# A graph attention block: tile 2 of the last head turned by DMA, one pool of banks, an x tile in another bank, and layer 2's own logits by way of VectorE

## The chip, the cores and the metric

The kernel runs on one core of a Trainium2 chip. The metric is device microseconds of one execution; of several executions the median is compared. A core has five engines with instruction streams of their own: TensorE (PE in the profile; its weight loads are shown apart as PEld), VectorE (DVE), ScalarE (ACT), GpSimd (POOL) and SyncE (SP), which here issues most of the DMA transfers. The engines wait for one another by semaphores. Matrix products land in PSUM banks, from which ScalarE or VectorE take them to SBUF.

## The reference

Two graph attention layers over 512 nodes with 768 features, a residual and a layer norm. Layer 1 has 8 heads of 768 features, layer 2 has one. All is fp32.

```python
def gat_layer(x, W, a_s, a_d, b, edge_index, concat):
    h = (x @ W).reshape(n, H, C)
    alpha_s = einsum('nhc,hc->nh', h, a_s)
    alpha_d = einsum('nhc,hc->nh', h, a_d)
    e = leaky_relu(alpha_s[src] + alpha_d[dst], 0.2)
    m = segment_max(e, dst);  e = exp(e - m[dst])
    alpha = e / (segment_sum(e, dst)[dst] + 1e-16)
    out = segment_sum(h[src] * alpha[:, :, None], dst)
    return out.reshape(n, H * C) + b
h = elu(gat_layer(x, W1, a_src1, a_dst1, b1, edges, True))
out = gat_layer(h, W2, a_src2, a_dst2, b2, edges, True)
x = layernorm(x + out)
```

## The kernel before

The edges are counted once, by products of one-hot tiles (L804, L789, L830), into a dense 512x512 table `cnt`, in which an entry is the number of edges between two nodes. After that each head is dense: the projection x @ W1 of the head, a 512x512 table of logits by four tiles of 128 destination rows, a softmax weighted by the table, the product of the softmax with the projected features, ELU, and the head's share of the projection of layer 2, which is summed over heads into `h2`.

The large products are done with fewer multiplications than the plain form. By halves there are seven steps P1 to P7 per product, by thirds fifteen, P0 to P14. Each step multiplies sums of blocks (made by VectorE, ScalarE or by accumulating DMAs) into a PSUM bank, and its `empty` then moves the bank to SBUF, by a ScalarE copy or by a VectorE addition. Halves of the projections are at L445 (helper `product`), thirds at L527, the attention products at L1099 and, for the first and the last head, in `near_first` (L1139), which takes destination nodes 0 to 255 ahead of the others: its first steps P1 and P2 need the softmax of tiles 0 and 1 alone, and the sums of `right_sums` (L1072 to L1075) need all four tiles. An fp32 matmul runs as two passes, so a matmul of the code shows as two weight loads and two matmuls.

Order. Each engine executes its instructions in the order in which the program issues them. The order is written out by hand: while the matmuls of step n are issued, the functions listed in `plan[n]` are issued to the other engines. The last head has a `plan` of its own (L1406 to L1411).

The softmax tiles lie with destinations on the partitions and must be transposed into `PT` for the product with the features. Two ways exist. `turn` (L1020, L1021): four TensorE transpositions into a `tr` bank and a ScalarE copy into `PT`; the tile has then been scaled by `scale` (L1301, ScalarE; the reciprocal comes from VectorE, L1011 and L1012). `turn_out` and `turn_in`: ScalarE scales the tile (L1028) and parts its 4-byte words into two halves of 16 bits (L1031), SP issues a transposing DMA (L1033), and when it has landed ScalarE joins the halves in `PT` (L1036). In the last head tiles 0 and 1 go by DMA and tiles 2 and 3 by TensorE.

PSUM. Banks come from pools and are taken in turn; a matmul that starts a new tile waits until the last reader of that bank's earlier tile is done. While the edges are counted there are a pool `mm0` of three banks and a pool `held` of two, used by P1 of the first projection and its overlays; afterwards these are closed and one pool `mm` of five opens. `tr` has two banks, `bc` has one, first used by the warming matmuls at the start (L292) and later for the broadcast rows of logits.

The start. `turn_x` (L327, L328) transposes blocks of x by TensorE into a bank of `mm0` and copies them to `xT` by ScalarE. Four of these calls stand behind position 3 of the first projection; the bank of the third is freed by VectorE's L672. VectorE's L425 to L428 then make sums of x blocks.

Layer 2's logits. A row of 512 logits per kind, source and destination, is accumulated by TensorE into the bank `rows` at four positions of 32 partitions (L1535), then copied by ScalarE into `row2` (128x512, L1564). `pick` does two things with it: L1570 spreads the source row over all partitions, and L1572 collects the destination logits into four columns, one per tile of 128 nodes, by four matmuls whose weights are 128x128 blocks of `row2` and whose moving operand is one column of `picks`. VectorE copies the four columns to `own2` (L1575), and ScalarE needs them for the first tile of logits (L723). The VectorE addition L570, behind L1575 in VectorE's order, empties the bank that P4 of layer 2's projection waits for. `fold` (L1530) is VectorE work between them. L1626 is the final product.

Of the kernel before, what the change touches and what calls it, by code (L numbers as in the profile page):

```python
# [39 lines left out]
def gat_pass(  # L40
# [42 lines left out]
    ohp = counting.enter_context(tc.tile_pool(name="onehot", bufs=1))  # L83
    tr = ctx.enter_context(tc.tile_pool(name="tr", bufs=2, space=bass.MemoryType.PSUM))
    bc = ctx.enter_context(tc.tile_pool(name="bc", bufs=1, space=bass.MemoryType.PSUM))
    mm = counting.enter_context(tc.tile_pool(name="mm0", bufs=3, space=bass.MemoryType.PSUM))
    held = counting.enter_context(tc.tile_pool(name="held", bufs=2, space=bass.MemoryType.PSUM))

    def row_bcast(ap_row):
        return bass.AP(tensor=ap_row.tensor, offset=ap_row.offset, ap=[[0, P], [1, D]])  # L90
# [215 lines left out]
    ones = const.tile([P, 1], F32, name="ones")  # L306
    nc.vector.memset(ones, 1.0)

    picks = const.tile([P, 2], F32, name="picks")
    for j in range(2):  # L310
        nc.vector.tensor_reduce(picks[:, j:j + 1], ident.rearrange("p (j k) -> p k j", k=32)[:, j, :], axis=AX.X,
                                op=ALU.add)
    far = const.tile([P, 1], F32, name="far")
    nc.vector.memset(far, -NO_EDGE)
    tiny = const.tile([P, 1], F32, name="tiny")
# [4 lines left out]
    xT = keep.tile([P, DC, N], F32, name="xT")  # L320


    def turn_x(t, r):

        ps = mm.tile([P, 512], F32, name="mm")
        for k in range(HK):
            nc.tensor.transpose(ps[:, k * P:(k + 1) * P], x_sb[:, t, (r * HK + k) * P:(r * HK + k + 1) * P], ident)  # L327
        nc.scalar.copy(xT[:, r * HK:(r + 1) * HK, t * P:(t + 1) * P],  # L328
                       ps[:, :HALF].rearrange("p (k n) -> p k n", n=P))
# [322 lines left out]
    def first_projection(h, XA, B_, between):  # L652


        HS[h] = hs = hpool.tile([P, NT, D], F32, name="hs")
        new_alpha(h)
        bank = {}

        def step(p, over, i, out, op):
            def multiply():  # L660
                if over is None:
                    bank[p, i] = (held if p == "P1" else mm).tile([P, 512], F32, name="held" if p == "P1" else "mm")
                else:
                    bank[p, i] = bank[over, i]
                product(bank[p, i], XA, B_, p, i, over is None)

            def empty():
                ps, o = bank[p, i][:, :HALF], out(i)
                if op is None:
                    nc.scalar.copy(o, ps)  # L670
                else:
                    nc.vector.tensor_tensor(o, o, ps, op=op)  # L672
            return multiply, empty, op is not None

        steps = [
            ("P1", None, lambda i: hs[:, i, L], None),
            ("P2", None, lambda i: hs[:, i, L], ALU.add),
            ("P5", None, lambda i: hs[:, 2 + i, R], None),
            ("P3", "P5", lambda i: hs[:, i, R], None),
            ("P6", "P1", lambda i: hs[:, i, R], ALU.subtract),  # L680
            ("P7", "P1", lambda i: hs[:, 2 + i, R], ALU.subtract),
            ("P4", "P1", lambda i: hs[:, 2 + i, L], None),
        ]

        def firsts():
            for k in range(HK):
                if k == HK - 1:
                    between()
                for i in range(2):
                    if k == 0:  # L690
                        bank["P1", i] = held.tile([P, 512], F32, name="held")
                    nc.tensor.matmul(bank["P1", i][:, :HALF], XA["P1"][:, k, i * P:(i + 1) * P], B_["P1"][:, k, :],
                                     start=k == 0, stop=k == HK - 1, skip_group_check=True)

        items = [step(p, over, i, out, op) for p, over, out, op in steps for i in range(2)]
        for i, multiply in enumerate((firsts, lambda: None)):
            items[i] = (multiply, *items[i][1:])
        return items
# [66 lines left out]
    if not general:  # L765
# [76 lines left out]
                    done.add(t)  # L842


        turns = {3: [(2, 0), (3, 0), (2, 1), (3, 1)]}
        sums = const.tile([P, 2 * NT + 2], F32, name="sums")
        wholes = len(items)

# [14 lines left out]
        for n, batch in enumerate(batches):  # L863
            fresh = sorted({c // quarter for c in batch} - made)
            made.update(fresh)
            if n == 0:
                waiting = [lambda k=k: destinations(k) for k in fresh]
            else:
                first = ahead_of.get(n, [])
                head = 1 if n == 1 else len(waiting)  # L870
                here = None
                if n + 1 == len(batches):
                    (k,), (before, *rest) = fresh, waiting
                    before()
# [12 lines left out]
            items_here = max(wants[n] - pos if n < len(wants) else 0, 1)  # L887
            share = len(ahead) // (items_here + 1) if n == 0 else -(-len(ahead) // items_here)
            for f in masks:
                f()  # L890
            waiting, masks = [], []
            for f in extra.pop(n, []):
                f()
            while n < len(wants) and pos < wants[n]:
                if pos == wholes:
                    pairs = projection(1, XA, B1)
                    items += [(m, e, False) for m, e in pairs[:4]]
                multiply, empty, on_vector = items[pos]
                multiply()
                if on_vector:  # L900
                    waiting.append(empty)
                else:
                    empty()
                pos += 1
                for t, r in turns.get(pos, []):
                    turn_x(t, r)
                if pos == 1:
                    nc.scalar.activation(nidx, low, AF.Copy, bias=0.5)
                part = 0 if n == 0 and pos == 2 else share
                for c in ahead[:part]:  # L910
                    one_hot(c, True)
                del ahead[:part]
            for c in ahead:
                one_hot(c, True)
            if n == 2:
                turn_b1()
            if n == 0:
                ((k,),) = [sorted({c // quarter for c in batches[1]} - made)]
                made.add(k)
                destinations(k)  # L920
                waiting.pop()()
            uncounted += batch
            if n + 1 == len(batches):
                for t in range(NT):
                    half(t, 0)()
            if n == 2 or n + 1 == len(batches):
                count(uncounted, n > 2)
                uncounted = []
# [57 lines left out]
    counting.close()  # L986


    mm = ctx.enter_context(tc.tile_pool(name="mm", bufs=5, space=bass.MemoryType.PSUM))
    late = ctx.enter_context(tc.tile_pool(name="late", bufs=1))  # L990
    h2 = late.tile([P, NT, D], F32, name="h2")
    pass_ = late.tile([P, 2, 2 * TH], F32, name="pass")
# [310 lines left out]
    for h in range(H - 1):  # L1303
# [75 lines left out]
        else:  # L1379
# [14 lines left out]
            def sum_up(*names):  # L1394
                return [gsums[p] for p in names]

            def at(f, *args):
                return [lambda: f(*args)]
# [8 lines left out]
            if last:  # L1407
                plan = {0: finish[:1], 1: finish[1:] + sum_up("P12") + at(score, 0), 2: sum_up("P9", "P7"), 3: sum_up("P1"),
                        4: sum_up("P6") + at(scored, 0) + at(score, 1), 5: sum_up("P14"), 6: sum_up("P10") + at(scored, 1) + at(score, 2),
                        7: at(out_by_dma, 0) + sum_up("P5"), 8: sum_up("P11") + at(scored, 2) + at(score, 3), 9: at(out_by_dma, 1),  # L1410
                        10: at(scored, 3), 11: at(scale, 2) + sum_up("P3"), 12: third_sum + at(turn_in, 0) + at(scale, 3), 13: at(turn_in, 1)}  # L1411
                AA, lsums = left_sums(H - 1, pass_.rearrange("p j n -> p (j n)"))
                plan[13] += lsums[:2]
                plan[14] = lsums[2:3]
# [8 lines left out]
                for f in attend:  # L1423
                    also(13, f)
            for n, (multiply, empty) in enumerate(pairs):
                if last and n > 12:
                    turn(q[n - 11], n - 11)
                multiply()
                for f in plan.get(n, []):
                    f()  # L1430
# [97 lines left out]
    def fold(parts):  # L1528
        for part, i, op in parts:
            nc.vector.tensor_tensor(part, part, u2[:, i, :], op=op)  # L1530
# [31 lines left out]
        add_rows(al2[:, :, t], ident, t, slice(t * P, (t + 1) * P), False, True)  # L1562
    row2 = work.tile([P, N], F32, name="nr")
    nc.scalar.copy(row2, rows[:, :N])  # L1564
    fold(parts[:2])
    own = tr.tile([P, 512], F32, name="tr")

    def pick():
        BC[H] = bc.tile([P, 512], F32, name="bc")
        nc.tensor.matmul(BC[H][:, :N], picks[:, 0:1].to_broadcast([P, P]), row2, start=True, stop=True)  # L1570
        for t in range(NT):
            nc.tensor.matmul(own[:, t:t + 1], row2[:, t * P:(t + 1) * P], picks[:, 1:2], start=True, stop=True)  # L1572

    pairs[7][0](pick)
    nc.vector.tensor_copy(own2, own[:, :NT])  # L1575
# [105 lines left out]
```

## Time and profile before

| | us |
|---|---|
| runs | 615.61, 614.91, 615.52 |
| median | 615.52 |
| profiled execution | 615.07 |
| its span | 613.0 |
| PE busy | 604.9 (99% of the span) |
| DVE busy | 525.3 (86%) |
| ACT busy | 335.4 (55%) |
| POOL busy | 145.5 (24%) |
| granted TensorE clock, mean | 0.998 |

The span runs from the first to the last instruction of the record; the profiled execution's own time is 2.07 us more. In the timeline a row has the start, the busy time, the engine, the line, the operation with output and inputs, how many instructions it groups, and in brackets how long the engine stood idle before it and which instruction of which engine ended that idle time.

### The profile page before, as it was taken

What the parts mean: (1) busy time and instruction counts of PE and PEld (TensorE: products, weight loads), DVE (VectorE), ACT (ScalarE), POOL (GpSimd) and SP (SyncE); (2) the same over time, 40 slices, a digit from 0 to 9 for tenths busy, and PEclk for the clock granted to TensorE, in tenths of its full rate; (3) what the DMA queues carried; (4) which work ended last, traced back from release to release, by engine and by line L of the source; (5) the groups of instructions that cost most, each with busy time, mean ns of one, the idle gap of its engine ahead of it and who ended that gap; (6) DMA issues with size and microseconds to landing.
All of it is one profiled execution on the core that took longest, in us unless ns stands there. A gap on an engine that the chain in (4) does not pass through costs nothing.

```text
span 613.0 us, 8592 instructions
## 1 busy us (share of the span) xinstructions
PE 604.9 (99%) x2772; PEld 481.9 (79%) x2772; DVE 525.3 (86%) x1149; ACT 335.4 (55%) x628; POOL 145.5 (24%) x182
## 2 busy tenths in 40 slices
PE   9999999999999999999999999999999999999995
PEld 5665775558888888888888888888888888885553
DVE  7999889887999879977898879977898878978785
ACT  5669776803675165823766164932757056753360
POOL 3310101032431332422431332412342303110000
PEclk9999999999999999999999999999999999999999
DMA  8992949699999998999899999999789994790032
GB/s 293 317 214 56 292 83 314 142 330 313 209 170 242 254 240 210 151 313 255 184 179 240 235 249 227 144 324 223 177 193 204 299 284 70 165 262 4 18 78 81
DMA packets 107292, 126.24 MB, mean 206 GB/s; under 512 B 41526, under 2 KB 87530, under 8 KB 106474
## 3 DMA queue, kind: packets, MB, share of 16 engines
q1 hardware_dynamic: 74813, 90.24, 48.5%
q0 software_dynamic: 32064, 35.00, 36.7%
q8 instruction: 24, 0.39, 0.3%
q10 hardware_dynamic: 365, 0.40, 0.2%
q14 instruction: 26, 0.21, 0.1%
HBM read 97.22 MB, written 2.90 MB: 163 GB/s over the span
## 4 chain that ended last, share of the span: by engine, by line
PE 97%; DVE 2%; ACT 1%; issue 0%; DVEq 0%
PE mm L527 47%; PE mm L445 19%; PE mm L1099 18%; PE mm L1139 6%; PE mm L1626 3%; PE held L445 2%; PE bc L292 1%; DVE os L804 0%; PE tr L830 0%; DVE odw L789 0%; PE tr L1535 0%; DVE here L784 0%; ACT hs L484 0%; PE tr L1020 0%; PE mm L327 0%
## 5 line engine op out<-in xcount | busy, mean ns | idle before, releaser
L533 ACT ACTIVATE hs<-mm 128x512 f32<-128x512 f32 x30 | 17.9, 596 | 83.7 <-PE mm L527 83.3
L1099 PE MATMUL mm<-PT,hs 128*128 128x256 f32 x216 | 52.5, 379 | 0.0
L736 ACT ACTIVATE q<-q,nmax 128x512 f32<-128x512 f32 x32 | 23.1, 721 | 49.0 <-DVE nmax L732 48.9
L540 DVE TENSOR_TENSOR hs<-hs,mm 128x512 f32<-128x512 f32 x45 | 30.9, 687 | 18.5 <-PE mm L527 18.1
L1099 PEld LDWEIGHTS mm<-PT,hs 128*128 128x128 f32 x216 | 41.0, 190 | 5.8
L538 POOL DMA_DIRECT2D h<-pass x22 | 26.7, 1307 | 75.9 <-ACT pass L537 75.0
L540 DVE TENSOR_TENSOR h<-h,mm 128x512 f32<-128x512 f32 x56 | 38.3, 684 | 5.8 <-PE mm L527 5.6
L1036 ACT COPY PT<-zr 128x1024 uint16<-128x1024 uint16 x34 | 39.4, 1158 | 4.8 <-DMA zr<-nr 3.2
L527 PE MATMUL mm<-w2r,xT 128*128 128x256 f32 x160 | 37.8, 379 | 0.0
L527 PE MATMUL mm<-w2r,gT 128*128 128x256 f32 x160 | 37.0, 379 | 0.0
L1099 PE MATMUL mm<-pS,gS 128*128 128x256 f32 x144 | 37.0, 379 | 0.0
L136 POOL DMA_DIRECT2D w1t<-in_L_gnn_W_dram x18 | 30.1, 1970 | 25.8 <-DVE pS L1072 25.8
L527 PE MATMUL mm<-w1t,hs 128*128 128x256 f32 x144 | 34.1, 380 | 0.0
L527 PE MATMUL mm<-w1r,hs 128*128 128x256 f32 x144 | 34.0, 379 | 0.0
L527 PE MATMUL mm<-w1r,gS 128*128 128x256 f32 x144 | 34.0, 379 | 0.0
L527 PEld LDWEIGHTS mm<-w2r,xT 128*128 128x128 f32 x160 | 30.4, 190 | 4.1
L527 PEld LDWEIGHTS mm<-w2r,gT 128*128 128x128 f32 x160 | 30.4, 190 | 4.1
L136 POOL DMA_DIRECT2D w1r<-in_L_gnn_W_dram x12 | 14.5, 1208 | 80.4 <-DMA w1r<-in_L_gnn_W_dram 45.7
L527 PEld LDWEIGHTS mm<-w1t,hs 128*128 128x128 f32 x144 | 27.3, 190 | 3.9 <-ACT absent L537 0.2
L1099 PEld LDWEIGHTS mm<-pS,gS 128*128 128x128 f32 x144 | 27.4, 190 | 3.7
L527 PEld LDWEIGHTS mm<-w1r,gS 128*128 128x128 f32 x144 | 27.3, 190 | 3.7
L527 PEld LDWEIGHTS mm<-w1r,hs 128*128 128x128 f32 x144 | 27.2, 190 | 3.8
(328 smaller groups left out, 1555.4 us busy)
## 6 DMA issues: line engine op xcount, KB each, us to landing
w2r<-in_L_gnn_W_dram SPq DMA_DIRECT2D x48, 384.0 KB
w1r<-in_L_gnn_W_dram SPq DMA_DIRECT2D x43, 384.0 KB
w1t<-in_L_gnn_W_dram SPq DMA_DIRECT2D x24, 256.0 KB
h<-pass POOLq DMA_DIRECT2D x22, 256.0 KB, 6.6
gT<-xd SPq DMA_DIRECT2D x5, 1024.0 KB
w1t<-in_L_gnn_W_dram POOLq DMA_DIRECT2D x18, 256.0 KB, 6.8
a_s<-in_L_gnn_a_src_dram SPq DMA_DIRECT2D x8, 384.0 KB
a_d<-in_L_gnn_a_dst_dram SPq DMA_DIRECT2D x8, 384.0 KB
```

Of the source, the lines that this page charges most:

```text
L136: nc.gpsimd.dma_start(o, i, accum_op=ALU.add)
L292: nc.tensor.matmul(idle[:, :cols], zeros[:, :P], zeros[:, :cols], start=True, stop=True)
L445: nc.tensor.matmul(ps[:, :HALF], A_[p][:, k, i * P:(i + 1) * P], B_[p][:, k, :], start=start and k == 0, stop=k == HK - 1, skip_group_chec ...
L527: nc.tensor.matmul(bank[chain][:, i * TH:(i + 1) * TH], A_[p][:, k, i * P:(i + 1) * P], B_[p][:, k, :], start=first and i == k == 0, stop= ...
L533: nc.scalar.activation(out(o), ps, AF.Copy, scale=sign)
L538: nc.gpsimd.dma_start(out(o), part, accum_op=ALU.add)
L540: nc.vector.tensor_tensor(out(o), out(o), ps, op=ALU.add if sign > 0 else ALU.subtract)
L736: nc.scalar.activation(q, q, AF.Exp, bias=nmax, scale=-1.0, accum_out=dens[t])
L1036: nc.scalar.copy(PT.rearrange("p s n -> p (s n)").bitcast(U16).rearrange("p (s n h) -> p s n h", s=NT, h=2)[:, :, t * P:(t + 1) * P, :], p ...
L1099: nc.tensor.matmul(bank[p][:, :HN], A_[p][:, k, c * P:(c + 1) * P], B_[p][:, k, :], start=over is None and k == 0, stop=k == 1, skip_group ...
L1139: nc.tensor.matmul(banks[c, p][:, :HN], A_[p][:, k, c * P:(c + 1) * P], B_[p][:, k, :], start=over is None and k == 0, stop=k == 1, skip_g ...
L1626: nc.tensor.matmul(ps[:, :cols.stop - cols.start], PT[:, s, t * P:(t + 1) * P], h2[:, s, cols], start=(s == 2), stop=(s == 1))
```

## The change

Five edits.

1. The pools `mm0` and `held` become one pool `mm` of five banks, which stays open to the end; the pool that was opened after the counting is gone.
2. In the last head, tile 2 goes by `out_by_dma` and `turn_in`, not by `scale` and `turn`. Tile 3's `scale` moves ahead of the join of tile 0. Tile 3 is still turned by TensorE, at step 14, and the join of tile 2 stands behind its copy.
3. In layer 2, VectorE transposes `row2` in squares of 32x32 into `squares`, and L1572 becomes four matmuls with `fours` (128x32) as weights and four columns of `squares` as the moving operand, each at another position of 32 columns of the array.
4. The third of the four calls of `turn_x` takes its tile from `bc`.
5. `picks`, two VectorE reductions at the start, becomes `fours`, one reduction.

```diff
-    mm = counting.enter_context(tc.tile_pool(name="mm0", bufs=3, space=bass.MemoryType.PSUM))
-    held = counting.enter_context(tc.tile_pool(name="held", bufs=2, space=bass.MemoryType.PSUM))
+    mm = ctx.enter_context(tc.tile_pool(name="mm", bufs=5, space=bass.MemoryType.PSUM))
...
-    picks = const.tile([P, 2], F32, name="picks")
-    for j in range(2):
-        nc.vector.tensor_reduce(picks[:, j:j + 1], ident.rearrange("p (j k) -> p k j", k=32)[:, j, :], axis=AX.X,
-                                op=ALU.add)
+    fours = const.tile([P, SQ], F32, name="fours")
+    nc.vector.tensor_reduce(fours, ident.rearrange("p (j k) -> p k j", k=SQ), axis=AX.X, op=ALU.add)
...
-    def turn_x(t, r):
+    def turn_x(t, r, pool=None):
-        ps = mm.tile([P, 512], F32, name="mm")
+        ps = mm.tile([P, 512], F32, name="mm") if pool is None else pool.tile([P, 512], F32, name="bc")
...
-                    bank[p, i] = (held if p == "P1" else mm).tile([P, 512], F32, name="held" if p == "P1" else "mm")
+                    bank[p, i] = mm.tile([P, 512], F32, name="mm")
...
-                        bank["P1", i] = held.tile([P, 512], F32, name="held")
+                        bank["P1", i] = mm.tile([P, 512], F32, name="mm")
...
-        turns = {3: [(2, 0), (3, 0), (2, 1), (3, 1)]}
+        turns = {3: [(2, 0), (3, 0), (2, 1, bc), (3, 1)]}
...
-    mm = ctx.enter_context(tc.tile_pool(name="mm", bufs=5, space=bass.MemoryType.PSUM))
...
-                        10: at(scored, 3), 11: at(scale, 2) + sum_up("P3"), 12: third_sum + at(turn_in, 0) + at(scale, 3), 13: at(turn_in, 1)}
+                        10: at(scored, 3), 11: at(out_by_dma, 2) + sum_up("P3"), 12: third_sum + at(scale, 3) + at(turn_in, 0), 13: at(turn_in, 1)}
...
-                if last and n > 12:
-                    turn(q[n - 11], n - 11)
+                if last and n == 14:
+                    turn(q[3], 3)
+                    turn_in(2)
...
     row2 = work.tile([P, N], F32, name="nr")
     nc.scalar.copy(row2, rows[:, :N])
+    squares = work.tile([P, N // SQ, SQ], F32, name="nr")
+    nc.vector.transpose(squares.rearrange("p b k -> p (b k)"), row2)
     fold(parts[:2])
     own = tr.tile([P, 512], F32, name="tr")
 
     def pick():
         BC[H] = bc.tile([P, 512], F32, name="bc")
-        nc.tensor.matmul(BC[H][:, :N], picks[:, 0:1].to_broadcast([P, P]), row2, start=True, stop=True)
-        for t in range(NT):
-            nc.tensor.matmul(own[:, t:t + 1], row2[:, t * P:(t + 1) * P], picks[:, 1:2], start=True, stop=True)
+        nc.tensor.matmul(BC[H][:, :N], fours[:, 0:1].to_broadcast([P, P]), row2, start=True, stop=True)
+        for g in range(P // SQ):
+            nc.tensor.matmul(own[g * SQ:(g + 1) * SQ, :NT], fours, squares.rearrange("p (t g) k -> p g t k", t=NT)[:, g, :, 1],
+                             start=True, stop=True, tile_position=(0, g * SQ), skip_group_check=True)
```

More of the change, by code (lines that the diff above doesn't have):

```diff
@@ L904, in gat_pass @@
                 pos += 1
-                for t, r in turns.get(pos, []):
-                    turn_x(t, r)
+                for t, r, *pool in turns.get(pos, []):
+                    turn_x(t, r, *pool)
                 if pos == 1:
```

## The prediction

> **What bounds the kernel now.** I read the head of the page first, then its chain that ended last, then the list of TensorE's waits, then the timeline around each of the four places that the change touches. Lines are those of the kernel before. The head and the chain:
>
> ```profile
> span 613.0 us, 8592 instructions
> PE 604.9 (99%) x2772; PEld 481.9 (79%) x2772; DVE 525.3 (86%) x1149; ACT 335.4 (55%) x628; POOL 145.5 (24%) x182
> PE 97%; DVE 2%; ACT 1%; issue 0%; DVEq 0%
> ```
>
> TensorE is busy 99% of the span and carries 97% of the chain, so time is won only where TensorE issues less or stops waiting. The other engines count where they hold TensorE up. The waits of its weight loads show how little is left to win:
>
> ```profile
> PEld tr L1535 <- issue: 1.7, 4, 0.5
> PEld tr L1572 <- issue: 0.5, 2, 0.2
> PEld mm L445 <- DVE h L570: 0.6, 1, 0.6
> PEld mm L753 <- DVE os L804: 0.5, 1, 0.5
> PEld mm L445 <- ACT hs L484: 0.4, 1, 0.4
> ```
>
> Columns: who waits for whom, microseconds in total, times, longest. Edits 1 and 3 meet rows of this list, edit 4 the row of L753; the turn of tile 2 removes TensorE work.
>
> **Edit 1, one pool of five banks.** Five banks taken in turn replace three (`mm0`) and two (`held`). This changes which earlier tile a new one has to wait for. In head 1's projection the first matmul of P6 needs a new bank at 48.64. Before, that bank's last reader is the ScalarE copy at 48.10; after, it is a tile emptied long ago, and the copy's bank is asked for only steps later.
>
> ```profile
> 47.91 0.60 PE L706 MATMUL tr<-ident,wide 128*128 128x128 f32 x4
> 48.10 0.48 ACT L484 COPY hs<-mm 128x384 f32<-128x384 f32 x1
> 48.63 3.52 PEld L445 LDWEIGHTS mm<-w2t,xS 128*128 128x128 f32 x12 [0.37 <-ACT hs L484]
> 48.64 3.81 PE L445 MATMUL mm<-w2t,xS 128*128 128x384 f32 x11
> ...
> 531.44 0.60 PE L1020 MATMUL tr<-ident,q 128*128 128x128 f32 x4
> 531.88 1.89 PE L527 MATMUL mm<-w1r,gS 128*128 128x256 f32 x8
> ```
>
> Four such transpositions hold TensorE 0.44 us, as 531.44 to 531.88 shows. So P6 could start at 47.91 + 0.44 = 48.35 and not at 48.64: 0.29 us. Upper end 0.37, the whole idle of the weight load; lower end 0, if another engine gives the time back later. The DVE has its own work up to then, but the next place where TensorE depends on it, head 0's attention at 74, leaves it idle (the row of 74.66 below). I take 0.29, the value from starts of matmuls. The pool adds two waits of TensorE on its own earlier matmuls, long done; I cost them at nothing, and TensorE's own order is their cover.
>
> **Edit 2, tile 2 by DMA.** TensorE loses one turn of the kind above: 0.44 us. In exchange, ScalarE scales (L1028) and parts halves (L1031) at 529.77, SP issues one more DMA transposition, and ScalarE joins the halves (L1036) after its copy of tile 3; it loses one copy at L1021. TensorE's P1 of the attention needs tiles 0 and 1 alone, so the question is when ScalarE, in its order, gets through.
>
> ```profile
> 525.63 4.78 SPq L1033 DMA_TRANSPOSE zr<-pS  x2
> 529.77 0.72 ACT L1301 ACTIVATE q<-q,rden 128x512 f32<-128x512 f32 x1
> 534.24 0.59 ACT L1021 COPY PT<-tr 128x512 f32<-128x512 f32 x1
> 535.25 0.90 POOL L274 DMA_DIRECT2D w1t<-w2t  x1 [7.65 <-DMA w1t<-in_L_gnn_W_dram]
> 536.65 0.68 DVE L1072 TENSOR_TENSOR pS<-PT 128x512 f32<-128x512 f32 x1
> 536.84 0.37 ACT L1145 COPY u<-mm 128x256 f32<-128x256 f32 x1 [2.00 <-PE mm L1139]
> 540.74 0.84 PEld L1139 LDWEIGHTS mm<-pS,pass 128*128 128x128 f32 x4
> 542.09 0.42 DVE L1169 TENSOR_TENSOR u<-u,mm 128x256 f32<-128x256 f32 x1 [1.36 <-PE mm L1139]
> ...
> 62.84 1.04 ACT L1031 COPY pS<-q 128x1024 uint16<-128x1024 uint16 x1
> 67.93 1.16 ACT L1036 COPY PT<-zr 128x1024 uint16<-128x1024 uint16 x1 [1.28 <-DMA zr<-pS]
> 74.66 0.42 DVE L1169 TENSOR_TENSOR u<-u,mm 128x256 f32<-128x256 f32 x1 [0.23 <-PE mm L1139]
> ```
>
> ScalarE: L1028 529.77 to 530.49, L1031 (1.04) to 531.55, tile 3's scale (0.72, at 531.88 as before) to 532.6, two joins of 1.16 (L1036) to 534.92, tile 3's copy (0.59) to 535.5, the new join to 536.7. Its next copy, L1145, is due at 536.84: covered, by 0.1. The landing: in head 0 the parted tile of 62.84 + 1.04 = 63.88 released its join at 67.93, 4.05 us later. From 531.55 that is 535.6, and the join could begin as late as 535.5 to 535.7 without delaying L1145. So I expect 0 to 0.1 us late, and DVE's L1072, which now waits for this join, at about 536.75 against 536.65. It is followed by L1073; TensorE needs that sum at 540.74, four microseconds on, and DVE has 1.36 idle before 542.09. Cost nothing; if the landing is later by x, x beyond some 0.5 us (the ScalarE copies are needed a matmul group later) reaches TensorE. SP's loads at L268 stand behind the transposition, and two took 4.78, so each queues 2.4; POOL's addition at 535.25, which waits for the first load, comes as much later, about 537.7. It feeds layer 2's weights, of which the first product stands past 550; I cost this at nothing, and past that cover at what it is late. Range of the edit: gain 0.44 to a loss of the landing's excess.
>
> **Edit 3, layer 2's own logits.** Four matmuls with 128 columns of weights and one moving column, in two passes each, become one VectorE transposition in 32x32 squares and four matmuls of 32 weight columns, at four positions of the array, with 4 moving columns.
>
> ```profile
> 569.33 0.40 PE L1535 MATMUL tr<-ident,al 128*2 128x128 f32 x8
> 569.66 0.94 PEld L445 LDWEIGHTS mm<-w2r,gT 128*128 128x128 f32 x4 [0.22 <-issue]
> 569.78 1.02 DVE L1530 TENSOR_TENSOR h<-h,pass 128x384 f32<-128x384 f32 x2
> 569.85 0.59 ACT L1564 COPY nr<-tr 128x512 f32<-128x512 f32 x1 [11.21 <-PE tr L1535]
> 571.91 0.95 PE L1572 MATMUL tr<-picks,nr 128*128 128x1 f32 x8
> 572.72 0.89 PE L445 MATMUL mm<-w2r,gT 128*128 128x384 f32 x2
> 572.90 0.16 DVE L1575 COPY own<-tr 128x4 f32<-128x4 f32 x1 [2.10 <-PE tr L1572]
> 573.57 3.52 PEld L445 LDWEIGHTS mm<-w1t,gT 128*128 128x128 f32 x12 [0.57 <-DVE h L570]
> ...
> L712 DVE STREAM_TRANSPOSE turned<-wide x7: 204/206/214, 88.3 to 500.7; 128x32 f32<-128x32 f32 x7
> ```
>
> L1572 holds TensorE from 571.91 to 572.72, 0.81 us. The nearest row for its successor is L1535: eight matmul passes at four positions, too, from 569.33 to the return at 569.66, 0.33 us. Add 0.10 before it for the entry, since the moves between shapes show up as idle "issue" there: 0.43. So L445 returns near 572.34, 0.38 us earlier. L1575 follows the last pass, not the return, and comes 0.5 earlier; L570 behind it releases P4's weights, now waited for 0.57. P4 then starts 0.48 earlier, between 0.38 and 0.57.
>
> The transposition must be cheap: it starts at 570.44, when ScalarE's row is there, ahead of the two folds (1.02) and L1575. 206 ns at 32 columns is about 0.15 for a tiny operation (L1575 took 0.16) and 0.05 for the columns; at 512 that is 0.16 + 16 x 0.05 = about 0.9, and the other 128x512 operations took 0.68 (L1072). With 0.7 to 0.9 the folds end at 572.2 to 572.4, where TensorE would release L1575 anyway. I take 0.48 us, with the ends 0.81 (all of the old block) and, if the 206 ns went 16 times, a loss worked out below. On the skill's side, the Trainium skill, "VectorE: DVE Perf Modes", section "The three transpose paths", gives 311 ns for a 128x128 VectorE transposition in bf16; four of them, 1.24 us as an estimate, would leave 0.2 us of this gain. No row here shows a transposition that wide.
>
> A rule of the Trainium skill speaks against this edit: "TensorEngine Tiling (Array Packing)", "Key Properties", says that a change of the tiling mode drains TensorE. The trace agrees, with 0.5 and 0.22 us of "issue" around L1535. By it the switch is paid twice; by the rows above that is in the 0.43 already.
>
> **Edit 4, an x tile in the warming bank.** The third of the four turns at 13.5 no longer waits for DVE's L672.
>
> ```profile
> 3.24 0.89 DVE L383 CAST idx_f<-idx_i 66x256 f32<-66x256 int32 x1 [0.96 <-DMA idx_i<-in_src_dram]
> ...
> 13.97 0.64 PEld L327 LDWEIGHTS mm<-ident,hs 128*128 128x128 f32 x6 [0.30 <-DVE hs L672]
> 14.00 1.42 ACT L328 COPY xT<-mm 128x384 f32<-128x384 f32 x3
> 14.56 0.86 ACT L328 COPY xT<-mm 128x384 f32<-128x384 f32 x2
> 15.45 0.96 DVE L425 TENSOR_TENSOR xS<-xT 128x768 f32<-128x768 f32 x1
> 28.33 0.14 PEld L753 LDWEIGHTS mm<-ident,b_rows 48*128 48x128 f32 x1 [0.55 <-DVE os L804]
> ```
>
> The third copy begins at 14.56, 0.56 after the second, where two copies take 0.86, so 0.43 each: 0.13 to 0.2 us are lost, and L425 waits for the last copy (14.56 + 0.86 = 15.42). It comes that much earlier. From there DVE is busy without a gap to 28.14, and TensorE waits 0.55 for it at 28.33. So this passes on as up to 0.2 us, or nothing if an operation in that stretch waits for something else. Ends 0 and 0.30 (the idle of the weight load). I take 0.2. Edit 5, one reduction for two, falls before DVE's idle of 0.96 at 3.24: nothing, and less than a microsecond were that idle gone.
>
> **The sum.** 0.29 + 0.44 + 0.48 + 0.20 = 1.41 us. The profiled execution took 615.07 (span 613.0 and 2.07 around it): it would take 613.66. The median of the three runs, 615.52, lies 0.45 above it: 614.1.
>
> **The rivals.** *Swallowed:* edits 1 and 4 only shift a wait, and edit 3 gives 0.2: 615.52 - 0.64 = 614.9. For it speaks that DVE is 86% busy and follows TensorE closely; against it, the idles of 0.23, 1.36 and 2.10 in the rows above.
> *Late transposition, the other side:* the new DMA queues behind the two before it or beside loads. Up to a landing at about 536.1 nothing happens; past it each microsecond stops ScalarE's L1145 and with it TensorE. The other three edits and the turn give 1.41, so it is slower than before past 537.5, by over 0.2% past 538.7. At 4.78, what the two take, the landing is at 536.3; at twice that, 541.1, the time is 614.1 + 5.0 = 619.1.
> *Squares dear:* 16 x 0.206 = 3.3 us puts L1575 at 570.44 + 3.3 + 1.02 = 574.8, 1.9 late: 615.52 - 0.93 + 1.9 = 616.5. From 1.4 us on, edit 3 loses. Against it: no 128x512 operation of DVE in the rows takes over 0.7.
> *Turns belong on TensorE:* same section of "VectorE: DVE Perf Modes" in the Trainium skill: 128x128 goes to TensorE. As a mechanism here it is the late transposition, with that time.
>
> **How the numbers follow.** 0.2% is 1.23 us, about what a measurement tells from no change. Forecast 0.58, its own range 613.6 to 614.6, four fifths of it below the bound of 614.3; swallowed 0.24, 614.6 to 615.3; late 0.07; squares dear 0.05; 0.06 for a delay that I don't see. Faster 0.46, same 0.39 (half of squares dear with it), slower 0.15. The range 613.3 to 615.7 leaves out the losses and goes below to about all terms at their upper ends (0.37 + 0.44 + 0.81 + 0.30 = 1.9).
>
> **What would show it.** P6's weights of head 1 no longer waiting at 48; no L1020 for tile 2, with the join's wait for its DMA near zero and L1145 near 536; VectorE's transposition at 0.7 to 0.9 us and P4's start 0.5 nearer to L1564's end; L425 0.2 nearer to L672, and L753 as well. Wrong it would be by a long wait of L1036, by a transposition over 1.4 us, or by those waits returning at the next release.

## The result, and the profile after

| | before | after |
|---|---|---|
| median, us | 615.58 (8 runs) | 613.55 (8 runs) |
| lowest and highest, us | 614.91, 616.82 | 612.83, 614.75 |
| profiled execution, us | 615.07 | 613.12 |
| its span, us | 613.0 | 611.3 |

The medians lie 2.03 us apart. By the estimate from all runs the changed kernel takes 0.9963 of the time before, with a 95% interval of 0.9952 to 0.9975, which is 1.5 to 3.0 us less. On another occasion, with ten runs beside twenty-one of the kernel before, the medians were 613.16 and 615.26, the ratio 0.9959 (0.9944 to 0.9973).

Line numbers after the change are three or four smaller than before up to layer 2's logits; so L524 is L527 of before, L442 is L445, L1135 is L1139, L1032 is L1036. In a row that groups several instructions the second number runs from the start of the first to the end of the last, with the gaps between them. The head of the page and the chain of the changed kernel:

```profile
span 611.3 us, 8588 instructions
PE 603.5 (99%) x2768; PEld 481.5 (79%) x2768; DVE 525.9 (86%) x1149; ACT 336.2 (55%) x629; POOL 145.5 (24%) x182
PE 99%; DVE 0%; ACT 0%; issue 0%; DVEq 0%
```

TensorE issues four instructions fewer and is busy 1.4 us less. DVE's and ScalarE's shares of the chain, 2% and 1% before, are now 0%; they tell along which engine the chain was followed, not what was won, for 3% of the span would be 18 us. Where the time went shows when the same instruction of TensorE is set against itself in the two timelines:

| TensorE instruction | before | after | so far |
|---|---|---|---|
| transposed bias, L753 / L750 | 28.33 | 28.16 | -0.17 |
| P6 of head 1, L445 / L442 | 48.64 | 48.17 | -0.47 |
| thirds of the last head, L527 / L524 | 522.73 | 522.15 | -0.58 |
| behind tile 2's turn, L527 / L524 | 531.88 | 530.87 | -1.01 |
| behind the own logits, L445 / L442 | 572.72 | 571.16 | -1.56 |
| P4, L445 / L442 | 573.57 | 571.98 | -1.59 |
| final product, L1626 | 585.29 | 583.69 | -1.60 |

Between these places the difference stays what it is: no later wait takes anything back. The rows of the final product, before and after:

```profile
585.29 6.94 PE L1626 MATMUL mm<-h,PT 128*128 128x384 f32 x21
583.69 8.55 PE L1626 MATMUL mm<-h,PT 128*128 128x384 f32 x26
```

The rows of the changed kernel's timeline at the four places, edit 1 first:

```profile
47.73 0.60 PE L703 MATMUL tr<-ident,wide 128*128 128x128 f32 x4
47.94 0.48 ACT L481 COPY hs<-mm 128x384 f32<-128x384 f32 x1
48.06 3.53 PEld L442 LDWEIGHTS mm<-w2t,xS 128*128 128x128 f32 x12
48.17 4.04 PE L442 MATMUL mm<-w2t,xS 128*128 128x384 f32 x12
```

P6 starts 0.44 behind the transpositions while ScalarE's copy is still running, and its weights wait for nothing.

```profile
528.56 3.70 SPq L1029 DMA_TRANSPOSE zr<-pS  x2
529.96 1.04 ACT L1027 COPY pS<-q 128x1024 uint16<-128x1024 uint16 x1
530.87 1.89 PE L524 MATMUL mm<-w1r,gS 128*128 128x256 f32 x8
531.88 2.22 ACT L1032 COPY PT<-zr 128x1024 uint16<-128x1024 uint16 x2
532.35 0.54 SPq L267 DMA_DIRECT2D w1t<-in_L_gnn_W_dram  x1
532.59 0.60 PE L1016 MATMUL tr<-ident,q 128*128 128x128 f32 x4
534.48 1.16 ACT L1032 COPY PT<-zr 128x1024 uint16<-128x1024 uint16 x1
535.72 0.69 DVE L1068 TENSOR_TENSOR pS<-PT 128x512 f32<-128x512 f32 x1
535.82 0.37 ACT L1141 COPY u<-mm 128x256 f32<-128x256 f32 x1 [0.18 <-PE mm L1135]
536.94 0.90 POOL L273 DMA_DIRECT2D w1t<-w2t  x1 [9.91 <-PE mm L1135]
```

Edit 2: one turn is left (532.59). The join of tile 2 at 534.48 has no bracket, so it waits for no DMA: by then, 3.5 us after the end of the parting at 529.96 + 1.04 = 531.0, the tile has landed. ScalarE's next copy waits for TensorE, not the reverse.

```profile
569.45 0.71 DVE L1563 STREAM_TRANSPOSE nr<-nr 128x512 f32<-128x512 f32 x1 [0.60 <-ACT nr L1561]
570.04 1.02 PE L1569 MATMUL bc<-nr,fours 128*128 128x512 f32 x2
570.99 0.24 PE L1571 MATMUL tr<-nr,fours 128*32 128x4 f32 x8
571.16 0.91 PE L442 MATMUL mm<-w2r,gT 128*128 128x384 f32 x2
571.30 0.16 DVE L1575 COPY own<-tr 128x4 f32<-128x4 f32 x1 [0.23 <-PE tr L1571]
571.98 3.52 PEld L442 LDWEIGHTS mm<-w1t,gT 128*128 128x128 f32 x12 [0.52 <-DVE h L567]
```

Edit 3: VectorE's transposition takes 0.71 us. The broadcast ahead of the own logits took, in the kernel before, from its start in this row to 571.91, two passes of 0.43:

```profile
571.05 1.02 PE L1570 MATMUL bc<-nr,picks 128*128 128x512 f32 x2
```

So in the changed kernel it is over at about 570.04 + 0.86 = 570.90, and L1571 holds TensorE from there to 571.16, 0.26 us and not 0.81.

```profile
13.90 1.35 DVE L582 TENSOR_TENSOR w1t<-w1r 128x1152 f32<-128x1152 f32 x1
14.80 0.51 ACT L325 COPY xT<-mm 128x384 f32<-128x384 f32 x1
15.35 0.96 DVE L422 TENSOR_TENSOR xS<-xT 128x768 f32<-128x768 f32 x1
28.16 0.13 PEld L750 LDWEIGHTS mm<-ident,b_rows 48*128 48x128 f32 x1 [0.55 <-DVE os L801]
```

Edit 4: L422 starts at 15.35, just behind the end of the last copy of x (14.80 + 0.51 = 15.31) and 0.10 after DVE's own work before it is over (13.90 + 1.35 = 15.25); before, it started at 15.45, 0.03 and 0.12 behind these two. L750 still waits 0.55 for DVE, 0.17 earlier.

### The profile page after: what moved, and what is told of

The parts are those of the page before. It is cut to its first block, busy times and chain, and to the rows that moved or that the text cites. A ratio compares the mean times of both kernels' runs of the same rounds, so it can differ in the third digit from the quotient of the medians.

```text
span 611.3 us, 8588 instructions
## 1 busy us (share of the span) xinstructions
PE 603.5 (99%) x2768; PEld 481.5 (79%) x2768; DVE 525.9 (86%) x1149; ACT 336.2 (55%) x629; POOL 145.5 (24%) x182
## 4 chain that ended last, share of the span: by engine, by line
PE 99%; DVE 0%; ACT 0%; issue 0%; DVEq 0%
PE mm L524 47%; PE mm L442 22%; PE mm L1095 18%; PE mm L1135 6%; PE mm L1626 3%; PE mm L689 1%; PE bc L291 1%; PE mm L324 0%; PE tr L827 0%; PE tr L1532 0%; PE bc L1569 0%; DVE hs L1630 0%; PE bc L827 0%; DVE st L1632 0%; PE tr L386 0%; ACT hs L1647 0%
## 5 line engine op out<-in xcount | busy, mean ns | idle before, releaser
L1032 ACT COPY PT<-zr 128x1024 uint16<-128x1024 uint16 x35 | 40.4, 1156 | 1.8 <-DMA zr<-pS 1.5
L524 PE MATMUL mm<-w2r,xT 128*128 128x256 f32 x160 | 37.8, 379 | 0.0
L524 PE MATMUL mm<-w2r,gT 128*128 128x256 f32 x160 | 37.0, 379 | 0.0
L524 PE MATMUL mm<-w1t,hs 128*128 128x256 f32 x144 | 34.1, 380 | 0.0
L524 PE MATMUL mm<-w1r,hs 128*128 128x256 f32 x144 | 34.0, 379 | 0.0
L524 PE MATMUL mm<-w1r,gS 128*128 128x256 f32 x144 | 34.0, 379 | 0.0
L524 PEld LDWEIGHTS mm<-w2r,xT 128*128 128x128 f32 x160 | 30.4, 190 | 4.1
L524 PEld LDWEIGHTS mm<-w2r,gT 128*128 128x128 f32 x160 | 30.4, 190 | 4.1
L524 PEld LDWEIGHTS mm<-w1t,hs 128*128 128x128 f32 x144 | 27.3, 190 | 3.8 <-ACT absent L534 0.2
L524 PEld LDWEIGHTS mm<-w1r,gS 128*128 128x128 f32 x144 | 27.4, 190 | 3.7
L1099 ACT COPY u<-mm 128x256 f32<-128x256 f32 x18 | 6.7, 372 | 42.9 <-PE mm L1095 42.9
```

Source lines behind the costliest of these rows:

```text
L524: nc.tensor.matmul(bank[chain][:, i * TH:(i + 1) * TH], A_[p][:, k, i * P:(i + 1) * P], B_[p][:, k, :], start=first and i == k == 0, stop= ...
L1032: nc.scalar.copy(PT.rearrange("p s n -> p (s n)").bitcast(U16).rearrange("p (s n h) -> p s n h", s=NT, h=2)[:, :, t * P:(t + 1) * P, :], p ...
L1099: nc.scalar.copy(u, part("P1"))
```

## The experiments

**The four edits one by one.** Each was put alone on the kernel before; edit 5, which makes the `fours` that edit 3 needs, went with edit 3.

```diff
-    mm = counting.enter_context(tc.tile_pool(name="mm0", bufs=3, ...))
-    held = counting.enter_context(tc.tile_pool(name="held", bufs=2, ...))
+    mm = ctx.enter_context(tc.tile_pool(name="mm", bufs=5, ...))
```

> Edit 1 alone on the kernel before. Theory (each edit's gain is local and is carried to the end): P6 of head 1's projection (L445, 48.64 before) starts 0.30 us earlier, and since its weights are then loaded ahead, its second matmul another 0.10; TensorE keeps 0.40 us to the end, and the time falls by 0.4 us. Rival (swallowed): the 0.40 us are gone again by head 0's attention, some 25 us later. If the 0.24 us that the changed kernel also won outside the span belong to the pools, the time outside the span falls from 2.07 to 1.83 us in this run, and in the other three it stays.

```profile
48.13 0.60 PE L705 MATMUL tr<-ident,wide 128*128 128x128 f32 x4
48.56 1.13 PE L444 MATMUL mm<-w2t,xS 128*128 128x384 f32 x3
```

Median 614.79 against 615.30; ratio 0.9990 (0.9981 to 1.0000). P6 follows the transpositions at 0.43 and not at 0.73. Against before, TensorE's P6 moves by 0.29 and its second matmul by another 0.10, and both stay until 403 us. There its profiled execution, which took 618.29, loses 3.3 us in one piece. The rows of that place in its timeline:

```profile
404.87 1.16 ACT L1034 COPY PT<-zr 128x1024 uint16<-128x1024 uint16 x1 [2.65 <-DMA zr<-pS]
405.93 0.59 ACT L532 ACTIVATE hs<-mm 128x512 f32<-128x512 f32 x1
406.57 2.46 PEld L526 LDWEIGHTS mm<-w2t,xS 128*128 128x128 f32 x12 [3.53 <-ACT hs L532]
```

A transposing DMA of a middle head landed late, 12.1 us after SP issued it at 392.76; the join waited 2.65 us for it, the copy of a full bank stood behind the join in ScalarE's order, and TensorE stood 3.53 us for that bank. That is the mechanism of my late-transposition rival, at a place that the change doesn't touch, in an execution where edit 2 was not even made. The time outside the span stayed at 2.07 us, so it isn't the pools that shorten it.

```diff
-                        ... 11: at(scale, 2) + sum_up("P3"), 12: third_sum + at(turn_in, 0) + at(scale, 3), ...
+                        ... 11: at(out_by_dma, 2) + sum_up("P3"), 12: third_sum + at(scale, 3) + at(turn_in, 0), ...
-                if last and n > 12:
-                    turn(q[n - 11], n - 11)
+                if last and n == 14:
+                    turn(q[3], 3)
+                    turn_in(2)
```

> Edit 2 alone on the kernel before. Theory: one turn less on TensorE, 0.44 us earlier from 531.9 on and to the end; the join of tile 2 (L1036, the third of the last head) doesn't wait for its DMA, and the sum L1072 starts no later against TensorE's first matmul of L1139 than before. Rival (late transposition): the join waits, ScalarE's L1145 behind it too, and TensorE stands idle at P2 or P6 of L1139, by as much as the join is late beyond half a microsecond.

```profile
535.44 1.16 ACT L1036 COPY PT<-zr 128x1024 uint16<-128x1024 uint16 x1
535.72 5.34 PE L1139 MATMUL mm<-PT,hs 128*128 128x256 f32 x24
536.68 0.68 DVE L1072 TENSOR_TENSOR pS<-PT 128x512 f32<-128x512 f32 x1
```

Median 614.54; ratio 0.9986 (0.9976 to 0.9996). TensorE is 0.44 us earlier behind the removed turn, the join waits for no DMA, and L1072 starts at 536.68, 0.96 behind TensorE's first matmul of L1139 at 535.72. Before, it was 0.88, so the sum does start 0.08 later against TensorE, which the expectation had ruled out; nothing waits for it. And the time outside the span, which is 2.06 us in the mean of the 31 runs of the kernel before and 2.04 to 2.07 for the other three edits, is 1.80 here. A quarter of a microsecond of the gain lies there, and it comes with edit 2.

```diff
+    nc.vector.transpose(squares.rearrange("p b k -> p (b k)"), row2)
...
-            nc.tensor.matmul(own[:, t:t + 1], row2[:, t * P:(t + 1) * P], picks[:, 1:2], start=True, stop=True)
+            nc.tensor.matmul(own[g * SQ:(g + 1) * SQ, :NT], fours, squares...[:, g, :, 1], ..., tile_position=(0, g * SQ), ...)
```

> Edits 3 and 5 alone on the kernel before. Theory: VectorE's transposition takes 0.71 us and is hidden; TensorE's excursion at L1572 falls from 0.81 to 0.27 us and P4 starts 0.58 earlier; time less by 0.6 us. Rival (squares dear or drain): 0.2 us or less is left at P4.

```profile
572.85 1.26 PEld L443 LDWEIGHTS mm<-w1t,gT 128*128 128x128 f32 x5 [0.52 <-DVE h L568]
```

Median 614.59; ratio 0.9984 (0.9974 to 0.9994). P4 starts at 572.85 and not at 573.57; 0.14 of that came from the start of the execution, so edit 3 gives 0.58 us, and VectorE's 0.71 us are hidden, as the theory has it.

```diff
-        turns = {3: [(2, 0), (3, 0), (2, 1), (3, 1)]}
+        turns = {3: [(2, 0), (3, 0), (2, 1, bc), (3, 1)]}
```

> Edit 4 alone on the kernel before. Theory: the fourth copy of x (L328) ends about 0.1 us earlier, VectorE's L425 follows it and the chain of VectorE to 28 keeps it: TensorE 0.1 to 0.25 us earlier from 28.3 on and to the end. Rival (swallowed): no shift of TensorE after 30 us.

Median 614.94; ratio 0.9995 (0.9985 to 1.0005), no difference by the times. Its profile shows why this edit can be worth nothing. The rows of VectorE:

```profile
14.04 1.36 DVE L585 TENSOR_TENSOR w1t<-w1r 128x1152 f32<-128x1152 f32 x1 [0.32 <-DMA w1r<-in_L_gnn_W_dram]
15.31 0.95 DVE L425 TENSOR_TENSOR xS<-xT 128x768 f32<-128x768 f32 x1
```

L585 waited 0.32 us for weights, and L425 then started behind L585, not behind the copies of x. In seven of the fourteen profiles of this study the weights were late there, by 0.2 to 1.0 us. Of the other seven, the two without edit 4 (the kernel before, edit 3 alone) have L425 start 2.36 and 2.42 us after the first of the four turns; with edit 4 it is 2.19 us in four, and 2.38 in the fifth, where VectorE's own work ends after the copies. So edit 4 is worth about 0.2 us or nothing, by what else VectorE waits for.

The four medians fall by 0.51, 0.76, 0.71 and 0.36, together 2.3, where the whole change gives 2.0 to 2.1. Each of them is uncertain by some 0.6 us, so the times agree with edits that add up and don't show it. The traces do: 0.40, 0.44, 0.58 and 0.2 are 1.6 on TensorE, where the table of starts has 1.60 for all four.

**How late may tile 2 land?**

```diff
-        nc.sync.dma_start(parted[t]..., apart, transpose=True)
+        for _ in range(2 if again else 1):
+            nc.sync.dma_start(parted[t]..., apart, transpose=True)
```

> The changed kernel, with the transposing DMA of the last head's tile 2 sent twice to the same place, the second one after the first has landed. Theory (the landing is covered, with about half a microsecond to spare): the join waits for the second landing at about 537.2, ScalarE's first L1141 copy ends near 538.8 and not at 536.2, and TensorE, which needs it at 537.35 for P2, loses about 1.4 us (0.5 to 2.5). Rival (the landing doesn't matter, other work covers it): no loss, or under 0.3 us. The time outside the span stays at 1.83 us if it goes with the removed turn.

```profile
SPq L1030 <- DMA zr<-pS: 1.9, 1, 1.9
...
537.62 1.16 ACT L1033 COPY PT<-zr 128x1024 uint16<-128x1024 uint16 x1 [2.66 <-DMA zr<-pS]
539.10 2.86 PE L1136 MATMUL mm<-PT,hs 128*128 128x256 f32 x12 [1.20 <-ACT u L1142]
```

The first row is of SP's waits: the second sending waited 1.9 us for the first to land. It was issued at 534.5, 3.1 us after the first. This execution was 0.38 us behind the changed one before this place and 1.85 behind it: TensorE loses 1.47 us, near the 1.4 expected. The tile lands, in the changed kernel's time, at 537.62 - 0.38 = 537.24; so, if each microsecond past the cover costs one, a landing up to 537.24 - 1.47 = about 535.8 is free. The first landing, at 534.5 - 0.4 = 534.1 in that time, is taken as the changed kernel's. So the landing matters, and it has some 1.6 us to spare, 1.3 at the least by the start of the join at 534.48. The median was 614.97, against 613.55 of the changed kernel. The time outside the span stayed at 1.81.

**How dear may the squares be?**

```diff
-    nc.vector.transpose(squares.rearrange("p b k -> p (b k)"), row2)
+    for _ in range(2):
+        nc.vector.transpose(squares.rearrange("p b k -> p (b k)"), row2)
```

> The changed kernel, with VectorE's transposition of the logits issued twice. Theory (from 1.4 us on edit 3 loses): the second 0.71 us delays the two folds behind it, L1575 starts near 571.8 and not at 571.3, and P4 about 0.5 later; nearly all of edit 3's 0.58 us is gone. Rival (the folds and L1575 have room): P4 stays where it is, or moves by 0.2 at most.

```profile
570.12 1.46 DVE L1564 STREAM_TRANSPOSE nr<-nr 128x512 f32<-128x512 f32 x2 [0.60 <-ACT nr L1561]
572.40 0.15 DVE L1576 COPY own<-tr 128x4 f32<-128x4 f32 x1
573.07 1.91 PEld L442 LDWEIGHTS mm<-w1t,gT 128*128 128x128 f32 x7 [0.94 <-DVE h L567]
```

The copy of the own logits has no bracket any more: VectorE is behind, not TensorE. This execution ran 0.67 late up to here (569.45 became 570.12), so P4 is 573.07 - 571.98 - 0.67 = 0.42 later. Of edit 3's 0.58, 0.16 is left. At 1.46 us the transposition has nearly used up what the edit gives; if each further tenth costs a tenth, the edit is even at about 1.6 us, not at the 1.4 of the prediction. The median was 613.79.

**Why was the excursion shorter than L1535's?**

```diff
-            nc.tensor.matmul(own[g * SQ:(g + 1) * SQ, :NT], fours, squares...[:, g, :, 1], ...)
+            nc.tensor.matmul(own[g * SQ:(g + 1) * SQ, :P], fours, squares...[:, g], ...)
```

> The changed kernel, with 128 moving columns and not 4 in each of the four matmuls of L1571; L1575 picks the four wanted columns afterwards. Theory (I sized the excursion by L1535's, whose passes move 128 columns, and that was the whole error): the excursion of TensorE grows from 0.27 to about 0.42 us, 0.1 to 0.2 more, and P4 with it. Rival (the excursion is the change of the array's shape, whatever moves): no more than 0.05.

```profile
570.84 0.42 PE L1571 MATMUL tr<-nr,fours 128*32 128x128 f32 x8
571.20 0.30 PEld L442 LDWEIGHTS mm<-w2r,gT 128*128 128x128 f32 x2 [0.20 <-issue]
```

From 570.84 to 571.20 it is 0.36 us, where four moving columns took 0.17 (570.99 to 571.16); against the instructions before, P4 moved by 0.18. With the 0.09 ahead of L1571, which stays, the excursion is 0.45 with 128 moving columns and 0.26 with 4. So the moved columns make the difference, and the row that I took, with 128 of them, was the wrong neighbour for 4. The median was 613.47.

**What does leaving the full shape cost by itself?**

```diff
-        nc.tensor.matmul(asked[0][:1, :2 * NT + 2], ones, sums, start=True, stop=True)
+        nc.tensor.matmul(asked[0][:, :2 * NT + 2], ones.to_broadcast([P, P]), sums, start=True, stop=True)
```

> The changed kernel, with the weights of the sum over partitions in head 0 (L644, two passes, ten moving columns) widened from 1 to 128 columns, so that the array keeps its shape; of the result the one row is used as before. In the changed kernel TensorE's L442 before it would be followed at 65.59 and L442 behind it starts at 65.81, with its second matmul 0.43 and not 0.32 later: 0.33 us in all. Theory (leaving and re-entering the 128-column shape costs about 0.2 of that, because weights can't be loaded ahead): 0.22 us are left, as for two passes of a transposition, so 0.1 less, and the idle of 0.55 before the weights disappears. Rival (it is the small matmul itself): no change, within 0.03.

The rows of the changed kernel and then of this one:

```profile
65.68 0.09 PEld L644 LDWEIGHTS bc<-sums,ones 128*1 128x1 f32 x2 [0.55 <-ACT nr L1027]
65.81 1.26 PEld L442 LDWEIGHTS mm<-w2r,xS 128*128 128x128 f32 x5
```

```profile
65.45 0.51 PEld L644 LDWEIGHTS bc<-sums,ones 128*128 128x128 f32 x2
65.88 1.27 PEld L442 LDWEIGHTS mm<-w2r,xS 128*128 128x128 f32 x5
```

With the full shape the weights are loaded while the matmul before still runs, the idle of 0.55 is gone, and everything behind is 0.10 us earlier (0.18 behind the changed kernel's execution before this place, 0.08 after it). It was a single run, of 613.59, but the trace of the candidate below, which has the same edit, shows the same 0.10. This is the cost of the change of shape: the weights on both sides of it aren't loaded ahead. The bracket names a ScalarE copy as releaser of the 0.55; since the wait left with the shape, it was not that copy.

**Does the spread of the runs come from late joins?** Both kernels spread over some 2 us from run to run, more than the whole change gives.

```diff
-                if n in (1, 2, 4):
-                    turn_in((n + 2) // 2)
+                if n in (2, 3, 5):
+                    turn_in({2: 1, 3: 2, 5: 3}[n])
```

> The changed kernel, with the joins of tiles 1, 2 and 3 in heads 1 to 6 one step of the projection by thirds later on ScalarE (after steps 2, 3 and 5, not 1, 2 and 4). Theory (the spread of the runs comes from transposing DMAs that land late now and then, and hold ScalarE's copies of the banks up behind their joins, as in the profile of edit 1 alone): the fastest runs stay, the slow tail of the spans (612 to 613 us) gets shorter, and the median falls by 0.2 to 0.8 us. Rival (the spread comes from elsewhere): median and spread as in the changed kernel; a loss if VectorE's sums of softmax tiles are late for the attention.

The median of seven runs was 613.33, with spans of 611.0 to 613.2: neither shorter nor less spread than the changed kernel's. So late joins don't make the spread alone. The profile was of the slowest run, and its 1.9 us lie ahead of 11 us, where no softmax tile is joined yet. The weight loads there, and those of the changed kernel:

```profile
8.07 0.33 PEld L689 LDWEIGHTS mm<-w1r,xT 128*128 128x128 f32 x1 [0.31 <-issue]
8.71 0.33 PEld L689 LDWEIGHTS mm<-w1r,xT 128*128 128x128 f32 x1 [0.31 <-issue]
...
30.02 0.14 PEld L750 LDWEIGHTS mm<-ident,b_rows 48*128 48x128 f32 x1 [0.55 <-DVE os L801]
```

```profile
7.02 1.80 PEld L689 LDWEIGHTS mm<-w1r,xT 128*128 128x128 f32 x6 [0.20 <-ACT xT L325]
```

In the slower start one load of weights takes 0.33 us and they come 0.64 apart; in the other six take 1.80, so 0.32 apart with single loads of 0.19. TensorE ran at half its pace for some microseconds there, after its first x tile had come 0.25 us later (5.16, not 4.91). That lateness isn't the cause by itself: in the profiles of the doubled landing and of the full shape the tile came at 5.18 and 5.22, and their loads are 0.32 apart from the first. From L750 on, that execution took as long as the changed kernel's: 613.2 - 30.02 = 583.2, against 611.3 - 28.16 = 583.1.

**A candidate, and the changed kernel beside it.** The later joins and the widened sum together, with the edits of the last two experiments.

> The changed kernel with the later joins and the widened sum over partitions together. Theory: 0.1 us from the second and 0.2 us or less at the median from the first, so 0.1 to 0.3 us under the changed kernel, hardly to be told by the times; rival: no faster, or slower where a join has become late for the attention.

> The changed kernel once more, beside the next one on the same chip. The ratio to the kernel before should come out near 0.9963 again.

The candidate's median is 613.30 and its ratio 0.9968 (0.9956 to 0.9979); the changed kernel's, on the same chip, 613.16 and 0.9959 (0.9944 to 0.9973). No difference can be told. The 0.10 us that the trace shows for the wider sum is a twentieth of what one run differs from the next.

**What of edit 2 shortens the time outside the span?**

```diff
-                    turn(q[3], 3)
+                    for _ in range(2):
+                        turn(q[3], 3)
```

> The changed kernel, with the last head's tile 3 turned twice by TensorE (four more transpositions and one more ScalarE copy). Theory for the span: TensorE 0.44 us later from there on. For the 0.24 us outside the span: if they hang on the length of TensorE's program (four matmuls fewer in edit 2), the time outside the span is back at 2.06 us; if on something else of edit 2 (the DMA, ScalarE's order), it stays near 1.82.

TensorE is 0.44 us later from there on, and the time outside the span stays at 615.03 - 613.2 = 1.83. It was a single run, but no run of any kernel strays by more than some 0.1 us there. So it doesn't hang on the length of TensorE's program. What of edit 2 makes it, the DMA or the order on ScalarE, stays open.

## Why the prediction was right, and where its sizes were off

The forecast of 614.1 was right in direction and in mechanism: each of the four terms is there on TensorE, edit 4's where the weights aren't late, and each is carried to the end. The measured 613.55 lies in its range and just under the likeliest case's own (613.6 to 614.6). That it lies in the range is partly luck: all terms at their upper ends, 1.9 us, come to 613.6 from the median of 615.52, the range went 0.3 below that, and the gain was as large as this only with a term that the sum didn't have. By the trace the terms were:

| term | predicted | measured |
|---|---|---|
| edit 1 | 0.29 | 0.40 |
| edit 2, on TensorE | 0.44 | 0.44 |
| edit 3 | 0.48 | 0.58 |
| edit 4 | 0.20 | 0.2, or 0 in executions whose weights are late |
| outside the span | 0 | 0.25 |
| sum | 1.41 | 1.7 to 1.9 |

*Edit 1.* I counted the wait from the starts of the matmuls and left out that after a wait the next weights aren't loaded ahead, so the second matmul is late by another 0.10. Even my upper end, the 0.37 of idle before the load, lacked it. That DVE and ScalarE give nothing back held.

*Edit 2.* The order on ScalarE came out as worked out, but earlier: the join begins at 534.48, where I had 535.5. I had kept tile 3's scaling at its old place, though edits 1 and 4 ahead of it move it up, and it began at 531.25; and I laid ScalarE's instructions end to end, while in the rows each begins about 0.1 before the one ahead of it ends. The landing took at most 3.5 us from the parting and not 4.05, and its room is some 1.6 us where I gave it half a microsecond. I misread a row: the two transpositions of 525.63 didn't take 4.78, for in that stretch SP mostly waited for ScalarE's second parting, and each held SP for about 1.26 us. So the 2.4 of delay for each, and the landings at 536.3 and 541.1 with the time of 619.1 in the late rival, have no row behind them. SP's loads and POOL's addition were later against the rest all the same, by luck about as much as said: SP waited for the third parting, until 531.0, the loads went at 532.35 and not at 530.51, and POOL's addition came at 536.94, with 1.0 us gained, where I had 537.7. Its bracket names TensorE, but it follows the first load's issue by 4.6 us, as before by 4.7. Nothing waited for it. The 0.25 outside the span was no term of my sum; I took what lies around the span as fixed.

*Edit 3.* The excursion was mis-sized, at 0.43 for 0.26. The nearest row by the number of passes and positions, L1535, was not the nearest by moved columns; with 128 of them 0.43 would have been near, at 0.45. The time of the transposition, 0.7 to 0.9, came out at 0.71. The estimate of 1.24 us from the Trainium skill's "VectorE: DVE Perf Modes" was too long by three quarters for this form. The change of shape costs 0.10 us net at L644, and at L1571 it was inside the excursion as I had put it. The drain at a change of mode that the Trainium skill's "TensorEngine Tiling (Array Packing)" names, under "Key Properties", agrees with that 0.10, if leaving the full 128 columns of weights is such a change.

*Edit 4.* Right in size where it counts, but I had not seen that a second wait, for the weights of L585, ends as late in half of the profiles.

*The rivals.* Swallowed: no, the table of starts shows nothing given back. Squares dear: no, and its break-even is nearer to 1.6 us than to 1.4, by the doubled transposition. Late transposition: not here; but the chain of it is real. It cost 1.47 us when the landing was doubled, and 3.3 us in a middle head in one execution of edit 1 alone. Turns belong on TensorE: not this one, for with edit 2 alone TensorE is 0.44 us earlier. The rule that 128x128 goes to TensorE stands in the Trainium skill's "VectorE: DVE Perf Modes" under "Rules for kernel authors", not in the section that I named, and only for a result that may lie in PSUM; here it has to be copied to SBUF.

## What to carry to other kernels

On an engine that is busy 99% of the time, price a removed wait by what the next instruction loses as well: behind a wait or a change of shape the following weights aren't loaded ahead, which is 0.10 us here. Choose the neighbouring row by the quantity that sets the duration (moved columns), not by the count of instructions. Effects of some tenths of a microsecond are read from the starts of the same instructions in two traces; the times alone, with 2 us from run to run, tell edits 2 and 3 from no change by little and leave edits 1 and 4 open.

## What the runs showed of the hardware that was not expected

- TensorE can run at half pace for some microseconds near the start (0.64 us between weight loads for 0.32), while the granted clock of those stretches reads 1.00. It was so in two of the fourteen profiles and made 1.4 and 1.9 us of their spans, 0.25 to 0.4 us of it by a first x tile that came later. In six of the other twelve the first transpositions of x are 0.21 us apart and not 0.11, which is the same pace for a shorter time. What starts and ends it was not tested.
- The time outside the span depends on the kernel: 2.06 us in the mean before, 1.83 after, within some 0.1 us from run to run. All of it comes with edit 2, and neither the pools nor four transpositions on TensorE change it.
- A transposing DMA can land late by microseconds in one execution, in a head that is the same in all of them, and ScalarE's order passes that on to TensorE: 2.65 us at the join, 3.53 at the bank. The profile of edit 2 alone has a smaller case in another middle head: the join waits 0.51 us at 192.25, and TensorE loses 0.32.
